# Two pairs of routed blocks at a time: one group of products a slot, and four blocks' weights in one tile

## The chip, the cores and the metric

One core of a Trainium2 chip runs the whole program. The metric is the device time of one execution in microseconds. Three runs of the kernel before took 1347.44, 1349.66 and 1351.03 us; the median, 1349.66 us, is the time to compare with. One further execution was profiled; every duration below is from it.

Engines are named as in the profile: PE is the matrix engine (PEld its weight loads), DVE the vector engine, ACT the scalar engine, POOL the general engine, SP the one that only issues transfers.

## What is computed

A transformer layer, once: attention between two layer norms, then a feed-forward layer with routed experts and a shared expert between two more. All of it is in float32.

```python
x = x + _layernorm(attn(_layernorm(x), wq, bq, wkv, bkv, wo))
x = x + _layernorm(ffn(_layernorm(x), gate_w, w_gate, w_up, w_down, sh_gate, sh_up, sh_down))
```

The input has 8 sequences of 512 rows of 256 values. Attention has 4 groups of 4 query heads of 128, with one key and one value head for each group, and a causal mask. The feed-forward layer is where the change lies:

```python
scores = softmax(x @ gate_w.T)                 # 64 experts
topk_w, topk_idx = top_k(scores, 6)
# expert e takes at most CAP = 64 of the rows that chose it, in order: buf[e] is 64 x 256
g = silu(einsum('ech,ehf->ecf', buf, w_gate))  # f = 176
u = einsum('ech,ehf->ecf', buf, w_up)
d = einsum('ecf,efh->ech', g * u, w_down)
y = (d of each row's six experts, weighed by topk_w, 0 for rows over CAP)
y = y + silu(x @ sh_gate.T) * (x @ sh_up.T) @ sh_down.T
```

Each expert's block is 64 rows, so two experts make a pair of 128 rows, and there are 32 pairs. Three weights of an expert (256 x 176, 256 x 176 and 176 x 256) are 176 KB each.

## The kernel before

**The loop.** Attention runs over 128 heads `k`: 16 a sequence, a "head" being four query heads' share of one tile of rows (line 1450). The order of all instructions on PE, DVE, ACT, POOL and SP is the program's own order: it is written out by hand (`manual_schedule`, line 176), and nothing is reordered. In each head the loop takes, in this order: the score products 3 and 2 (`scores`, L566, with a reduction on DVE, L570, and an exponential on ACT, L574), the exchange of the head before (`turned`, two transposes on DVE, L602, then four transfers to DRAM and one back into `et`), score products 1 and 0, the weighing on POOL (`weigh`, L584), query products (`queries`, L426), the products with the values for the head two before (`mix`, L639, evicted by ACT at L650), side work of the feed-forward layer, and keys or values of the next group (`group_step`: nothing, keys, values, values for heads 0, 1, 2, 3 mod 4).

**The routed experts between.** The experts' work is a generator, `experts` (L1056), and the loop takes a step of it (`next(routed)`) at up to four places of a head, called slots here:

- slot a, after `turned(k - 1)` and before score products 1 and 0 (L1467)
- slot b, after the weighing and before the queries (L1496)
- slot c, after `mix` (L1521)
- slot d, at the end of the head, after `group_step` (L1557)

Slots b and c are open from head 94, a and d from head 97's end. The first steps build the tables of rows (`tables`); then `experts` goes over pairs `m`, with two steps an iteration. The first step of iteration m holds `start_pair(m)`, `down(m - 5)`, `gate_up(m - 3)`, `turn_hidden(m - 4)`, `load_gate_up(m - 1)` and `load_down(m - 3)`; the second holds `gate_up_hidden(m - 3)`, `scatter(m - 5)`, `turn_rows(m - 2)` and a step of `free_slots`. What they do for one pair:

| step | lines | what it issues |
|---|---|---|
| `start_pair` | 948 | POOL: an indirect gather of the pair's 128 rows into `gx` |
| `load_gate_up`, `load_down` | 958, 965 | ACT queue: three transfers of 352 KB into `wgu` and `wd` |
| `turn_rows` | 973-977 | PE: two transposes (`ptx`); DVE: copies `gxt`, `gw` |
| `gate_up` | 984, 987 | PE: products of 64 columns for the two experts, side by side (`pgu`); ACT: tanh into `hid` |
| `gate_up_hidden` | 993, 994 | DVE: two operations on `hid` and `pgu` |
| `turn_hidden` | 1001, 1003 | PE: two transposes (`pth`); DVE: copy `ht` |
| `down` | 1010, 1018 | PE: products of 64 columns (`pd`); ACT: two scaled copies into `dd` |
| `scatter` | 1021 | POOL: an indirect transfer that adds `dd` to `y_d` |

**Buffers.** PSUM has three pools here: `ps_s` with three banks, shared by `psc`, `ptx`, `pth` and some of the shared expert's products; `ps_m` with three banks, shared by `pq`, `pav`, `pk`, `pv`, `pd`, `pgu` and others (`bank`, L74); `ps_o` for the output sums. In SBUF, pool `p3` has two buffers of each tag, so `wgu` and `wd` each hold two pairs, and `gxt` and `ht` two; `gx` and `dd` have three, `gw` four. Tags `wgu` and `wd` are also used by `join_heads` early in the program, and by `finish` after the routed work.

**After the routed work.** When `experts` sets `pairs["all"]`, the loop turns to `finish_early`, which adds up, normalises and stores the first five sequences.

Of the kernel before, what the change touches and what calls it, by code (L numbers as in the profile page):

```python
# [11 lines left out]
F32 = mybir.dt.float32  # L12
# [7 lines left out]
P = 128  # L20
B, T, E = 8, 512, 256
NT = B * T
NI = T // P
# [4 lines left out]
G, QPG, D = 4, 4, 128  # L28
NH = G * QPG
NX, F, TOPK, CAP = 64, 176, 6, 64  # L30
FC = F // 2
NM = NX // 2
# [7 lines left out]
EARLY = 5  # L40
# [7 lines left out]
def sandwich_kernel(ctx, tc, x, wq, bq_t, wkv, bk_t, bv, wo, gate_wt, w_gate, w_up, w_down,  # L48
                    sh_gate_t, sh_up_t, sh_down_t, pe_t, out):
    nc = tc.nc  # L50
# [23 lines left out]
    def bank(shape, name):  # L74
        return ps_m.tile(shape, F32, tag="m", name=name)
# [43 lines left out]
    def on_act(dst, src):  # L119
        nc.scalar.copy(dst, src)  # L120
# [35 lines left out]
    with ExitStack() as part:  # L156
# [785 lines left out]
        table, pairs = {}, {}  # L942

        def start_pair(m):

            l = pairs[m] = {"m": m}
            l["gx"] = p4[0].tile([P, ROW], F32, tag="gx", name=f"gx_{m}")
            nc.gpsimd.indirect_dma_start(
                out=l["gx"], out_offset=None, in_=xg_d[:, :],
                in_offset=bass.IndirectOffsetOnAxis(ap=table["idx"][:, m, 0:1], axis=0))  # L950

        def load_gate_up(key):
            l, queue = pairs[key], nc.sync if key == "late" else nc.scalar
            m = l["m"]

            l["wgu"] = p3.tile([P, 2, 2, 2, F], F32, name=f"wgu_{key}", **l.get("wgu_at", {"tag": "wgu"}))
            for k, w in enumerate((w_gate, w_up)):
                queue.dma_start(out=l["wgu"][:, :, k, :, :].rearrange("p e c f -> p e (c f)"),
                                in_=w[ds(m * 2, 2)].rearrange("e (p c) f -> p e (c f)", p=P))

        def load_down(key):
            l, queue = pairs[key], nc.sync if key == "late" else nc.scalar
            m = l["m"]
            l["wd"] = p3.tile([FC, 2, 2, E], F32, name=f"wd_{key}", **l.get("wd_at", {"tag": "wd"}))
            queue.dma_start(out=l["wd"].rearrange("p e c h -> p e (c h)"),
                            in_=w_down[ds(m * 2, 2)].rearrange("e (p c) h -> p e (c h)", p=FC))

        def turn_rows(key):
            l = pairs[key]
            pt = ps_s.tile([P, 2, P], F32, tag="s", name=f"ptx_{key}")  # L970
            rows = l["gx"][:, :E].rearrange("s (p c) -> s c p", c=2)
            for c in range(2):
                nc.tensor.transpose(pt[:, c, :], rows[:, c, :], ident)
# [16 lines left out]
        def gate_up_hidden(key):  # L990
            l = pairs[key]
            pgu = l.pop("pgu")
            nc.vector.scalar_tensor_tensor(l["hid"], l["hid"], 1.0, pgu[:, 0, :], ALU.add, ALU.mult)
            nc.vector.scalar_tensor_tensor(l["hid"], l["hid"], 0.5, pgu[:, 1, :], ALU.mult, ALU.mult)

        def turn_hidden(key):
# [5 lines left out]
            l["ht"] = p3.tile([FC, 2, P], F32, tag="ht", name=f"ht_{key}")  # L1002
            on_dve(l["ht"], pt[:FC])

        def down(key):
            l = pairs[key]
            pd = bank([P, E], f"pd_{key}")
            for c in range(2):
                for e in range(2):
                    nc.tensor.matmul(pd[ts(e, CAP), :], lhsT=l["ht"][:, c, ts(e, CAP)],  # L1010
                                     rhs=l["wd"][:, e, c, :], start=c == 0, stop=c == 1)
            dd = l["dd"] = p4[0].tile([P, E], F32, tag="dd", name=f"dd_{key}")
            if key == "late":
                on_act(dd, pd)
                return
            for e in range(2):
                rows = slice(e * CAP, (e + 1) * CAP)
                nc.scalar.mul(dd[rows, :], pd[rows, :], l["gw"][rows, e : e + 1])
# [37 lines left out]
        def experts():  # L1056


            yield from tables()
            yield  # L1060
            later = free_slots()
            for m in range(NM + 5):
                if m < NM:
                    start_pair(m)
                for behind_, step in ((5, down), (3, gate_up), (4, turn_hidden), (1, load_gate_up), (3, load_down)):
                    if 0 <= m - behind_ < NM:
                        step(m - behind_)
                yield
                if 0 <= m - 3 < NM:
                    gate_up_hidden(m - 3)  # L1070
                if 0 <= m - 5 < NM:
                    scatter(m - 5)
                if 0 <= m - 2 < NM:
                    turn_rows(m - 2)
                if m >= 2:
                    next(later, None)
                if m == NM + 4:
                    pairs["all"] = True
                yield

        def output(b, y, x1):
# [14 lines left out]
        def finish(b, tags):  # L1096

            ys = [q.tile([P, NI, E], F32, tag=tag, name=f"y{n}_{b}") for n, (q, tag) in enumerate(tags[:2])]
# [3 lines left out]
            x1 = residual(b, *tags[2])  # L1102
# [301 lines left out]
        EARLY_TAGS = [(p3, "wgu"), (p3, "wd")]  # L1404

        FINISHED_AT = (1, 2, 5, 6, 8)

        def finish_early():

            rows = [finish(b, EARLY_TAGS + [[(p1, "xn"), (p2, "xnt")][b % 2]]) for b in range(EARLY)]  # L1410

            def at(n, mixed):
                for b, first in reversed(list(enumerate(FINISHED_AT))):
                    if first <= n <= first + 3 if mixed else n in (first, first + 2):
                        next(rows[b])

            return at
# [32 lines left out]
        for k in range(NK):  # L1450
            b, s = divmod(k, NH)
# [76 lines left out]
            if k == FIRST_FREE:  # L1528

                work = table["work"]  # L1530
                table["rest"] = nc.values_load(work[0:1, 0:1], min_val=0, max_val=NM - 1)
                table["m"] = nc.values_load(work[0:1, 1:2], (ET.DVE, ET.SP), min_val=0, max_val=NM - 1)
                pairs["late"] = {"m": table["m"], "wgu_at": {"tag": "wgu_late", "bufs": 1},
                                 "wd_at": {"tag": "wd_late", "bufs": 1}}
                load_gate_up("late")
            if k == FIRST_FREE + 2:
                load_down("late")
# [36 lines left out]
        with tc.For_i(0, table["rest"], 1) as n:  # L1574
            m = nc.values_load(table["work"][0:1, ds(n + 2, 1)], (ET.DVE, ET.SP), min_val=0, max_val=NM - 1)
# [82 lines left out]
```

## Time and profile before

| what | us |
|---|---|
| median of three runs | 1349.66 |
| the profiled execution, its own time | 1346.28 |
| its span, first to last instruction | 1344.6 |
| first routed load issued / last `pd` product | 892.7 / 1167.0 |
| one `pd` product, one `pgu` product (mean length) | 0.38 / 0.46 |
| one `ht` copy, one `gxt` copy on DVE | 0.42 / 0.42 |
| one `tanh` on ACT, one scaled copy `dd` | 0.32 / 0.47 |

The granted clock of PE was 0.997 over the execution. A product's length runs from its start to its modelled end, and products overlap, so the time that one takes from the next is the distance between their starts: some 0.22 us for a 128x256 instruction of `pav` (0.38 us long), of which a float32 product has two. In the page's first part an engine's share is busy time over the span. In a timeline each line is a start, a length, the engine, the line of the kernel, the operation, what it writes and reads, its shape and how many were merged; in brackets stands idle time before it and what ended it.

### The profile page before, as it was taken

How to read it: one execution, taken by the hardware profiler on the slowest of the kernel's cores; microseconds unless marked ns; L12 is line 12 of the kernel's file. 1: busy time of each engine (PE TensorE's matmuls, PEld its weight loads, DVE VectorE, ACT ScalarE, POOL GpSimd, SP SyncE). 2: the span in 40 equal slices, each digit the busy share in tenths (PEclk: the TensorE clock that was granted, in tenths of full speed). 3: DMA queues.
4: the chain of work that ended last, by engine and by line, in shares of the span. 5: the costliest groups of instructions: out<-in, count | busy, mean ns of one | idle time of the engine just before them, and what ended most of it. 6: DMA issues, size and time to landing. Idle time of an engine off the chain costs nothing. (4 is left out here: it accounts for less than half of the span.)

```text
span 1344.6 us, 21778 instructions
## 1 busy us (share of the span) xinstructions
PE 1319.8 (98%) x6746; PEld 1018.7 (76%) x6746; DVE 911.5 (68%) x2931; ACT 546.8 (41%) x1665; POOL 660.3 (49%) x1080
## 2 busy tenths in 40 slices
PE   9999999999999999999999999999999999999997
PEld 7877887888778887788778877876667676767774
DVE  5575577777887678777886778666656444567645
ACT  3333354334443454344433443434343334444523
POOL 4556463436452563446434643355545444477711
PEclk9999999999999999999999999999999999999999
DMA  8676677756775676566765667579999889777712
GB/s 268 176 219 208 201 215 219 205 185 211 220 218 174 201 226 213 177 209 204 224 193 162 204 189 202 171 213 303 307 284 281 246 239 299 182 239 262 234 36 72
DMA packets 160435, 285.53 MB, mean 212 GB/s; under 512 B 17292, under 2 KB 123437, under 8 KB 160317
## 3 DMA queue, kind: packets, MB, share of 16 engines
q1 hardware_dynamic: 122893, 212.14, 52.6%
q0 software_dynamic: 13328, 36.05, 9.1%
q10 hardware_dynamic: 24096, 35.92, 8.5%
q8 instruction: 55, 0.90, 0.3%
q14 instruction: 63, 0.52, 0.1%
HBM read 168.44 MB, written 115.61 MB: 211 GB/s over the span
## 5 line engine op out<-in xcount | busy, mean ns | idle before, releaser
L584 POOL TENSOR_SCALAR e<-e,recip 128x512 f32<-128x512 f32 (+1 forms) x504 | 245.3, 525 | 424.1 <-DVE recip L580 367.7
L574 ACT ACTIVATE e<-e,least 128x32 f32<-128x32 f32 (+1 forms) x504 | 258.5, 514 | 260.4 <-DVE least L570 235.1
L639 PE MATMUL pav<-et,v 128*128 128x256 f32 x1280 | 300.4, 382 | 11.5 <-DMA et<-ex_d 8.9
L639 PEld LDWEIGHTS pav<-et,v 128*128 128x128 f32 x1280 | 241.5, 191 | 52.8 <-issue 7.1
L566 PE MATMUL psc<-kt,qt 128*128 128x32 f32 (+15 forms) x1024 | 274.9, 407 | 0.9 <-DVE qt L431 0.4
L570 DVE CUSTOM_DVE_ANT_0 e<-psc,mask 128x32 f32<-128x32 f32 (+1 forms) x504 | 204.2, 430 | 96.4 <-PE psc L566 93.8
L650 ACT ACTIVATE ao<-pav,bv_sb 128x256 f32<-128x256 f32 x255 | 107.1, 471 | 368.5 <-PE pav L639 344.7
L566 PEld LDWEIGHTS psc<-kt,qt 128*128 128x128 f32 x1024 | 161.5, 191 | 59.4 <-issue 25.9
L602 DVE STREAM_TRANSPOSE eb<-e 128x1024 f32<-128x1024 f32 (+1 forms) x252 | 197.5, 822 | 2.0 <-POOL e L584 1.5
L1021 POOL DMA_INDIRECT y_d<-dd,idx x32 | 51.1, 1597 | 93.2 <-ACT e L574 27.2
L574 ACT ACTIVATION_READ_ACCUMULATOR e<-e,least 128x1 f32 x504 | 94.6, 188 | 0.0
L716 PEld LDWEIGHTS pc<-set,crossed 128*128 128x128 f32 x640 | 77.0, 192 | 4.9 <-issue 1.7
L716 PE MATMUL pc<-set,crossed 128*128 128x128 f32 x640 | 78.8, 276 | 0.6 <-POOL crossed L710 0.6
L426 PE MATMUL pq<-xnt,wq_sb 128*128 128x256 f32 x320 | 75.5, 380 | 0.0
L716 PEld LDWEIGHTS ps<-set,ao 128*128 128x128 f32 x480 | 59.9, 192 | 15.3 <-issue 7.4
L470 PE MATMUL pq_back<-rows_joined,heads 128*128 128x256 f32 x264 | 71.3, 379 | 0.0
L388 PEld LDWEIGHTS pv<-wkv_sb,xnt 128*128 128x128 f32 x512 | 65.9, 192 | 4.5 <-issue 1.1
L388 PE MATMUL pv<-wkv_sb,xnt 128*128 128x128 f32 x512 | 67.5, 275 | 0.5 <-ACT ao L650 0.5
L426 PEld LDWEIGHTS pq<-xnt,wq_sb 128*128 128x128 f32 x320 | 59.2, 190 | 9.2 <-issue 0.7
L379 DVE SCALAR_TENSOR_TENSOR kt<-pk,bk_sb,pe_sb 128x512 f32<-128x512 f32 x32 | 24.0, 750 | 60.5 <-PE pk L377 58.5
L470 PEld LDWEIGHTS pq_back<-rows_joined,heads 128*128 128x128 f32 x264 | 50.2, 190 | 16.2 <-issue 8.2
L377 PE MATMUL pk<-xnt,wkv_sb 128*128 128x512 f32 x128 | 60.2, 593 | 0.3 <-ACT xnt L120 0.3
(281 smaller groups left out, 2017.6 us busy)
## 6 DMA issues: line engine op xcount, KB each, us to landing
ex_d<-eb SPq DMA_DIRECT2D x504, 160.0 KB
et<-ex_d SPq DMA_DIRECT2D x126, 640.0 KB
wgu<-in_w_gate ACTq DMA_DIRECT2D x32, 352.0 KB
wgu<-in_w_up ACTq DMA_DIRECT2D x32, 352.0 KB
wd<-in_w_down ACTq DMA_DIRECT2D x32, 352.0 KB
set<-wc_d SPq DMA_DIRECT2D x20, 512.0 KB
set<-ws_d SPq DMA_DIRECT2D x20, 384.0 KB
y<-y_d POOLq DMA_DIRECT2D x10, 512.0 KB, 6.8
```

Of the source, the lines that this page charges most:

```text
L377: nc.tensor.matmul(pk, lhsT=wkv_sb[:, c, g, 0, :], rhs=s["xnt"][:, c, :], start=c == 0, stop=c == NC - 1)
L388: nc.tensor.matmul(pv[:, i, :], lhsT=s["xnt"][:, c, ts(2 * n + i, P)], rhs=wkv_sb[:, c, g, 1, :], start=c == 0, stop=c == NC - 1, skip_gro ...
L426: nc.tensor.matmul(pq[:, n, :, :], lhsT=wq_sb[g][:, c, ts(2 * pair + n, D)], rhs=seqs[b]["xnt"][:, c, :].rearrange("p (u v) -> p u v", v=P ...
L470: nc.tensor.matmul(out, lhsT=factor[0], rhs=factor[1], start=first, stop=last, skip_group_check=True)
L566: nc.tensor.matmul(psc[:, :w], lhsT=halves[k // 2][:, at, :, :].rearrange("d h t -> d (h t)"), rhs=seqs[b]["kt"][g][:, :w], start=True, st ...
L570: nc.vector.tensor_tensor_reduce(out=e, in0=psc[:, :w].rearrange("p (c t) -> p c t", t=BS), in1=mask[:, T - w :].rearrange("p (c t) -> p c ...
L574: nc.scalar.activation(e, e, AF.Exp, bias=l["least"][:, q : q + 1], scale=-1.0, accum_out=l["total"][:, q : q + 1])
L584: engine.tensor_scalar(e, e, recip[:, q : q + 1], 1.0, ALU.mult, ALU.mult)
L602: nc.vector.transpose(eb[:, :, first : first + count, :, :].rearrange("p a j r t -> p j a r t"), weighed[k % 2][:, end - count : end, :, : ...
L639: nc.tensor.matmul(pav[n // NI][:, :, n % 2, :], lhsT=seqs[b]["v"][g][:, j, :], rhs=et[:, :, first + j, :], start=j == 0, stop=j == count ...
L650: nc.scalar.activation(ao, pav[n // NI][:, :, n % 2, :], AF.Identity, bias=bias)
L716: nc.tensor.matmul(bank_[:, n, :], lhsT=a, rhs=w, start=pair == 0 and n == 0, stop=pair == 1 and n == len(factors[0]) - 1, skip_group_chec ...
```

## The change

The 32 pairs become 16 twos of pairs.

- **Steps and slots.** `experts` now loops over n with four steps an iteration. Step one: `gate_up_hidden` for both pairs of n - 1, and one scatter of n - 2. Step two: `turn_hidden` for both pairs of n - 1. Step three: the other scatter, `turn_rows` for both pairs of n, `start_pair` for both of n + 1. Step four: the down products of n - 1, the gate and up products of both pairs of n, then the loads of gate and up for n + 1 and of down for n. Two steps stand ahead of the loop.
- **Down products** of two pairs write one bank `pd` of 128x2x256; four scaled copies follow.
- **Weights** of four blocks stand in one tile, with one buffer of each tag; gate, up and down each come in one transfer of 704 KB from ACT's queue. The late pairs keep their own loads.
- **`join_heads` and `finish`** use halves of one tile in place of two buffers of a tag.

```diff
@@ join_heads
-            t = p3.tile([P, 4, 2, D], F32, tag="wgu" if g >= 2 else "wd", name=f"heads_{g}")
+            tag = "wgu" if g >= 2 else "wd"
+            if tag not in joined:
+                joined[tag] = p3.tile([P, 2, 4, 2, D], F32, tag=tag, name=f"heads_{tag}", bufs=1)
+            t = joined[tag][:, g % 2]
...
+        def load_gate_up_of_two(n):
+            t = p3.tile([P, 4, 2, 2, F], F32, tag="wgu", name=f"wgu_{n}", bufs=1)
+            for k, w in enumerate((w_gate, w_up)):
+                nc.scalar.dma_start(out=t[:, :, k, :, :].rearrange("p e c f -> p e (c f)"),
+                                    in_=w[ds(n * 4, 4)].rearrange("e (p c) f -> p e (c f)", p=P))
+            for at in range(2):
+                pairs[2 * n + at]["wgu"] = t[:, 2 * at : 2 * at + 2]
+
+        def load_down_of_two(n):
+            t = p3.tile([FC, 4, 2, E], F32, tag="wd", name=f"wd_{n}", bufs=1)
+            nc.scalar.dma_start(out=t.rearrange("p e c h -> p e (c h)"),
+                                in_=w_down[ds(n * 4, 4)].rearrange("e (p c) h -> p e (c h)", p=FC))
...
+        def down_products(l, pd):
+            for c in range(2):
+                for e in range(2):
+                    nc.tensor.matmul(pd[ts(e, CAP)], lhsT=l["ht"][:, c, ts(e, CAP)], rhs=l["wd"][:, e, c, :],
+                                     start=c == 0, stop=c == 1, skip_group_check=True)
...
+        def down_two(n):
+            pd = bank([P, 2, E], f"pd_{n}")
+            for at in range(2):
+                down_products(pairs[2 * n + at], pd[:, at, :])
+            for at in range(2):
+                l = pairs[2 * n + at]
+                dd = l["dd"] = p4[0].tile([P, E], F32, tag="dd", name=f"dd_{2 * n + at}")
                 for e in range(2):
+                    rows = slice(e * CAP, (e + 1) * CAP)
+                    nc.scalar.mul(dd[rows, :], pd[rows, at, :], l["gw"][rows, e : e + 1])
...
@@ experts
-            for m in range(NM + 5):
-                if m < NM:
-                    start_pair(m)
-                for behind_, step in ((5, down), (3, gate_up), (4, turn_hidden), (1, load_gate_up), (3, load_down)):
-                    if 0 <= m - behind_ < NM:
-                        step(m - behind_)
...
+            two(0, start_pair)
+            yield
+            once(0, load_gate_up_of_two)
+            yield
+            for n in range(NM // 2 + 2):
+                two(n - 1, gate_up_hidden)
+                once(n - 2, lambda n: scatter(2 * n))
+                next(later, None)
                 yield
+                two(n - 1, turn_hidden)
+                yield
+                once(n - 2, lambda n: scatter(2 * n + 1))
+                two(n, turn_rows)
+                two(n + 1, start_pair)
+                next(later, None)
+                if n == NM // 2 + 1:
                     pairs["all"] = True
+                yield
+                once(n - 1, down_two)
+                two(n, gate_up)
+                once(n + 1, load_gate_up_of_two)
+                once(n, load_down_of_two)
                 yield
...
@@ finish_early
-            rows = [finish(b, EARLY_TAGS + [[(p1, "xn"), (p2, "xnt")][b % 2]]) for b in range(EARLY)]
+            both = [p3.tile([P, 2, NI, E], F32, tag=tag, name=f"early_{tag}", bufs=1) for tag in ("wgu", "wd")]
+            rows = [finish(b, [t[:, b % 2] for t in both], [(p1, "xn"), (p2, "xnt")][b % 2]) for b in range(EARLY)]
```

(`two(n, step)` takes a step for pairs 2n and 2n + 1, `once(n, step)` takes it for n; both do nothing outside the 16 twos.)

More of the change, by code (lines that the diff above doesn't have):

```diff
@@ L952, in load_gate_up @@
         def load_gate_up(key):
-            l, queue = pairs[key], nc.sync if key == "late" else nc.scalar
-            m = l["m"]
-            l["wgu"] = p3.tile([P, 2, 2, 2, F], F32, name=f"wgu_{key}", **l.get("wgu_at", {"tag": "wgu"}))
+            m = pairs[key]["m"]
+            t = pairs[key]["wgu"] = p3.tile([P, 2, 2, 2, F], F32, tag="wgu_late", name=f"wgu_{key}", bufs=1)
             for k, w in enumerate((w_gate, w_up)):
-                queue.dma_start(out=l["wgu"][:, :, k, :, :].rearrange("p e c f -> p e (c f)"),
-                                in_=w[ds(m * 2, 2)].rearrange("e (p c) f -> p e (c f)", p=P))
+                nc.sync.dma_start(out=t[:, :, k, :, :].rearrange("p e c f -> p e (c f)"),
+                                  in_=w[ds(m * 2, 2)].rearrange("e (p c) f -> p e (c f)", p=P))
@@ L961, in load_down @@
         def load_down(key):
[L962 to L966, printed above, removed]
+            m = pairs[key]["m"]
+            t = pairs[key]["wd"] = p3.tile([FC, 2, 2, E], F32, tag="wd_late", name=f"wd_{key}", bufs=1)
@@ new lines, in load_down @@
+            nc.sync.dma_start(out=t.rearrange("p e c h -> p e (c h)"),
+                              in_=w_down[ds(m * 2, 2)].rearrange("e (p c) h -> p e (c h)", p=FC))
+        def load_gate_up_of_two(n):
[5 more added lines that the diff above has]
+                pairs[2 * n + at]["wgu"] = t[:, 2 * at : 2 * at + 2]
@@ L968, in turn_rows @@
+        def load_down_of_two(n):
[3 more added lines that the diff above has]
+            for at in range(2):
+                pairs[2 * n + at]["wd"] = t[:, 2 * at : 2 * at + 2]
         def turn_rows(key):
@@ L1007, in down @@
             pd = bank([P, E], f"pd_{key}")
-            for c in range(2):
-                for e in range(2):
[L1010 to L1018, printed above, removed]
+            down_products(l, pd)
+            l["dd"] = p4[0].tile([P, E], F32, tag="dd", name=f"dd_{key}")
+            on_act(l["dd"], pd)
+        def down_two(n):
+            pd = bank([P, 2, E], f"pd_{n}")
+            for at in range(2):
+                down_products(pairs[2 * n + at], pd[:, at, :])
+            for at in range(2):
+                l = pairs[2 * n + at]
+                dd = l["dd"] = p4[0].tile([P, E], F32, tag="dd", name=f"dd_{2 * n + at}")
+                for e in range(2):
+                    rows = slice(e * CAP, (e + 1) * CAP)
+                    nc.scalar.mul(dd[rows, :], pd[rows, at, :], l["gw"][rows, e : e + 1])
         def scatter(m):
@@ L1061, in experts, with two, once @@
             later = free_slots()
-            for m in range(NM + 5):
-                if m < NM:
-                    start_pair(m)
-                for behind_, step in ((5, down), (3, gate_up), (4, turn_hidden), (1, load_gate_up), (3, load_down)):
-                    if 0 <= m - behind_ < NM:
-                        step(m - behind_)
-                yield
[L1069 to L1077, printed above, removed]
-                    pairs["all"] = True
+            def two(n, step):
+                if 0 <= n < NM // 2:
+                    for at in range(2):
+                        step(2 * n + at)
+            def once(n, step):
+                if 0 <= n < NM // 2:
+                    step(n)
+            two(0, start_pair)
[6 more added lines that the diff above has]
+                next(later, None)
+                yield
+                two(n - 1, turn_hidden)
[5 more added lines that the diff above has]
+                if n == NM // 2 + 1:
+                    pairs["all"] = True
+                yield
[3 more added lines that the diff above has]
+                once(n, load_down_of_two)
                 yield
@@ L1094, in output, with finish @@
             yield
-        def finish(b, tags):
-            ys = [q.tile([P, NI, E], F32, tag=tag, name=f"y{n}_{b}") for n, (q, tag) in enumerate(tags[:2])]
+        def finish(b, ys, room):
             for k in range(2):
@@ L1101, in finish @@
                 yield
-            x1 = residual(b, *tags[2])
+            x1 = residual(b, *room)
             for i in range(NI):
@@ L1401, in last_output @@
                     nc.sync.dma_start(out=rows_of(out, b * T)[:, i - 1 : i + 1, :], in_=x1[:, i - 1 : i + 1, :])
-        EARLY_TAGS = [(p3, "wgu"), (p3, "wd")]
         FINISHED_AT = (1, 2, 5, 6, 8)
         def finish_early():
-            rows = [finish(b, EARLY_TAGS + [[(p1, "xn"), (p2, "xnt")][b % 2]]) for b in range(EARLY)]
+            both = [p3.tile([P, 2, NI, E], F32, tag=tag, name=f"early_{tag}", bufs=1) for tag in ("wgu", "wd")]
+            rows = [finish(b, [t[:, b % 2] for t in both], [(p1, "xn"), (p2, "xnt")][b % 2]) for b in range(EARLY)]
             def at(n, mixed):
@@ L1532, in sandwich_kernel @@
                 table["m"] = nc.values_load(work[0:1, 1:2], (ET.DVE, ET.SP), min_val=0, max_val=NM - 1)
-                pairs["late"] = {"m": table["m"], "wgu_at": {"tag": "wgu_late", "bufs": 1},
-                                 "wd_at": {"tag": "wd_late", "bufs": 1}}
+                pairs["late"] = {"m": table["m"]}
                 load_gate_up("late")
```

## The prediction

> **What bounds the kernel now.** I read the page's busy shares first, then the routed stage in stretches of time (columns: stretch, length, busy time and instructions of PE, PEld, DVE, ACT, POOL, granted clock, DMA share, GB/s), then who waited for whom on PE, then the routed tiles, then one head's timeline.
>
> ```profile
> PE 1319.8 (98%) x6746; PEld 1018.7 (76%) x6746; DVE 911.5 (68%) x2931; ACT 546.8 (41%) x1665; POOL 660.3 (49%) x1080
> ...
> 880.00:1172.00 292.00, 287.86 (x1573) 200.46 (x1572) 163.14 (x555) 114.89 (x332) 143.52 (x177) 1.00 0.89 263
> ...
> 940.00:980.00 40.00, 39.00 (x205) 26.30 (x202) 22.33 (x69) 14.93 (x40) 19.83 (x24) 1.00 0.99 305
> ...
> PE pav L639 <- DMA et<-ex_d: 2.8, 2, 1.8
> ```
>
> TensorE sets the end: 98% over all, 287.9 of 292 us in the routed stage, where its only named waits above 1 us are two for `et` (2.8 us together). The DMA engines come second, full from 940 to 980. VectorE is at 56%, but its order is written by hand, so its place in a chain can matter although its share doesn't. So a term counts if it changes PE's own time or makes PE wait.
>
> PE and then DVE around one step between two heads (start, duration, what, count):
>
> ```profile
> 1015.00 1.08 PE L1010 MATMUL pd<-wd,ht 88*64 88x256 f32 x8
> 1015.92 1.35 PE L984 MATMUL pgu<-wgu,gxt 128*64 128x352 f32 x8
> 1017.20 0.46 PE L1001 MATMUL pth<-ident,hid 128*88 128x128 f32 x2
> 1017.50 0.76 PE L566 MATMUL psc<-kt,qt 128*128 128x160 f32 x4
> 1018.18 0.51 PE L973 MATMUL ptx<-ident,gx 128*128 128x128 f32 x2
> 1018.52 1.40 PE L566 MATMUL psc<-kt,qt 128*128 128x352 f32 x4
> ...
> 1018.04 0.31 DVE L570 CUSTOM_DVE_ANT_0 e<-psc,mask 128x160 f32<-128x160 f32 x1
> ...
> 1018.30 0.36 DVE L570 CUSTOM_DVE_ANT_0 e<-psc,mask 128x192 f32<-128x192 f32 x1
> ...
> 1018.58 1.57 DVE L602 STREAM_TRANSPOSE eb<-e 128x1024 f32<-128x1024 f32 x2
> 1020.07 0.30 DVE L993 SCALAR_TENSOR_TENSOR hid<-hid,pgu 128x176 f32<-128x176 f32 x1
> 1020.40 0.34 DVE L994 SCALAR_TENSOR_TENSOR hid<-hid,pgu 128x176 f32<-128x176 f32 x1
> 1020.66 0.42 DVE L123 COPY gxt<-ptx 128x256 f32<-128x256 f32 x1
> ...
> 1021.06 0.52 DVE L570 CUSTOM_DVE_ANT_0 e<-psc,mask 128x352 f32<-128x352 f32 x1
> ```
>
> Two things are to be seen. The score and transpose outputs share three PSUM banks in turn (pool `ps_s`), so each needs the bank of the one three places earlier: `ptx` at 1018.18 needs that of `pth`, and starts just after `ht` was copied out. And DVE puts the 1.57 us transpose L602 between the second and third score reduction. Today the last two score products don't mind: their banks are those of the first two, reduced before L602. They run underneath it.
>
> **Slots.** The steps are taken four at a time in a head k: a (between scores 2 and 1), b (before the queries), c (after `mix`), d (end). Counting yields, old and new both begin after six table slots and end in head 115. Before, down and gate/up products of one pair stand in b and d of each head; afterwards those of two pairs stand in c alone, `gate_up_hidden` in d, `turn_hidden` in a, `turn_rows` in b.
>
> **1. Fewer groups of half-width products.** From the starts of consecutive PE instructions in the trace: the full-width instruction before `pd` lasts 94 ns longer to the next start than its like (523 for 429 ns), the first `pd` pair 51 longer, the last `pgu` 101 longer (389 for 288), the first `pth` 78 longer (187 for 109; `pth_late`, which follows no such group, has none). 0.324 us a group. There are 34 groups (30 joint, 2 of gate/up alone, 2 of down alone), then 17: 17 x 0.324 = **-5.5 us**. The products themselves stay: 0.21 us per `pd` pair of instructions, 0.29 per `pgu` pair.
>
> **2. Slot a: the wait that takes their place.** PE's order becomes psc3, psc2, pth, pth, psc1, psc0 on three banks. psc0 needs the bank of the first `pth`, hence its copy `ht`, and DVE's order is reduce 3, reduce 2, L602, `ht`, `ht`. From the start R of reduce 3, psc0 can start at R + (reductions 0.26 to 0.76 by width) + 1.49 + 0.42 + 0.05. PE has only psc1 (0.5 to 0.8 us) and the transposes (0.11 each) to do meanwhile. Any of the three banks is released only behind L602, so another rotation would not help.
>
> R is late too. Let T be the end of the last `pgu`. ACT first copies four `dd` (0.95 a pair, from 0.25 after `pd`, thus until T-0.2), then two `tanh`; the second can't start before T+0.18. DVE's two `hid` pairs (0.65 each) then end at T+1.5; where the key product stands between (heads 2 mod 4) its `kt` (0.75, ready at T+1.9) comes first and they end at T+3.9. DVE reduces only after that. Ends of psc0, less PE's pure work, less what the old slot a lost anyway (elapsed time between psc3's start and psc0's end, against its products):
>
> - heads 1 mod 4 (no keys or values between): 4.58 - 2.33 - 0.37 = 1.9
> - 2 mod 4 (keys): 7.04 - 4.00 - 0.20 = 2.8
> - 3 mod 4 (values 0.87): 4.75 - 3.12 - 0.13 = 1.5
> - 0 mod 4 (values): 4.56 - 3.13 - 0.64 = 0.8
>
> 7.0 for four heads, and slot a carries `turn_hidden` in the 16 heads 99 to 114: **+28 us**. If `hid` is never late, R follows psc3 alone: 0.75 + 1.1 + 1.4 + 0.4 = 3.65 for four, +14.6: the lower bound. Above, 32 (side steps' DVE work ahead of `hid`). Behind psc0 on PE stands all of the head, so nothing gives it back but the 2.8 us of waits for `et`.
>
> Here a rule speaks against the change: the Trainium skill (Perfetto Trace Analysis, Optimization Strategy) reads a gap that repeats on the saturated engine as too little PSUM or SBUF for the next tile. By the row, the three `ps_s` banks cost 2.9 us in 12 of today's `ptx`; by the rule, two more transposes between scores on the same three should make it a regular bubble, of a size it doesn't tell.
>
> **3. Banks of the other pool.** Slot c takes all three `ps_m` banks: `pd`, `pgu`, `pgu`. The second `pgu` needs that of `pav`: two ACT evictions, 0.84 us together, against 2.9 us of products before it. Keys or values need that of `pd`: four `dd` end 2.2 us after it, PE comes at 2.4. Taken at **0**; covered by 2.1 and 0.2 us, and 0.2 x 16 = 3 us if the last slips.
>
> **4. Weights.** Transfers from ACT go from 96 to 48 of twice the size, bytes and run lengths alike. ACT's issue takes 374 to 482 ns each, at times up to 1704; ACT is 39% busy, and PE's next need of it is half a head away: 0. But one buffer for four blocks means that the loads start only after the last `pgu` of the slot, and `wd`, last in its queue, is wanted first. Counting the queue's bytes in the trace, now gate and up land 3.1 to 7.8 us after the first issue, the second 1.1 us behind the first, and `wd` 2.1 to 5 behind that; all are there 1.9 to 13 us ahead of use. Doubled: up + 2 x 1.1 + 2 x (wd - up) = 9.6 to 16.8, mean 12.3 (an estimate). They are wanted at interval - 4.3 (the products of slot c) + the stalls of 2. Intervals between ends of `mix` are 13.5 to 21.8, first 11.1: wanted after 10.5 to 20. A wait of some 3 us at the first load, 1 us in six or seven short heads. Bounds 0 and 15; I take **+5**, the lower half, as DMA gains from every pause of PE.
>
> The Trainium skill (DMA: Bandwidth & Descriptors, Anatomy of one DMA; Rules for kernel authors) gives a software-issued transfer a fixed 2 us and asks for 1 MiB or more in one. By that, 48 transfers fewer would save 96 us of transfer time; by this trace no product waits for a weight, and the saving is nothing.
>
> **5. The rest at nothing.** 32 gathers and 32 scatters stay; POOL issues two gathers in a row in b, about 1.0 us each, with half of POOL's time free. `join_heads` and the early `finish` write the same bytes into parts of one tile instead of two; their readers and the order are the same. No PE wait stands there to be had, so no gain either.
>
> **Sum.** -5.5 + 28 + 0 + 5 = +27.5. On the profiled execution's 1346.28 (span 1344.6 and 1.7 around it) 1373.8; that execution lies 3.4 below the median of the runs, so on 1349.66: **1377 us**, slower by 2%.
>
> **Rivals.**
> - *Faster*: the wait in slot a doesn't arise and only the 5.5 us remain, 1344. For: DVE is 56% busy, and every step is still there one slot ahead of its user. Against: it needs L602 and `ht` within psc1's time, 1.95 us in at most 0.8. It decides below that point. 9%, with a tenth of no change beside it (4%).
> - *`hid` is in time* (other PE work in d hides it): -5.5 + 14.6 = +9, 1359. Against: heads 1 mod 4 have nothing between. 18%.
> - *Weights bind*: the 2.1 MB burst lands at 12.3 to 16.8 after T in most heads, each waits 1 to 2 us more than taken, +43 with the other terms, 1393. For: DMA at 0.99 from 940 to 980. Against: PE's new pauses lengthen the head. 12%.
> - *The group isn't one group*: the second `pgu` waits for `pav`'s eviction, the saving is gone, +33, 1383. Against: 2.1 us of cover. 5%.
> - *Forecast*: 52%; its own range runs from +14.6 - 5.5 - 2.8 = +6 to 32 - 5.5 + 15 = +42.
>
> Three runs spread over 0.27%, so 0.3% is what this kernel's measurement tells from no change. Faster 9%, same 4%, slower 87%. The range of 8 in 10 leaves out the fast case and the top of the weights': 1357 to 1393.
>
> **What would show it.** Step 1: 17 starts of `pgu` groups with 16 products each, each preceded by `pd`. Step 2: psc0 starting within 0.1 us of the end of the first `ht` copy in every head 99 to 114, and idle PE of 1 to 3 us there; psc0 right behind psc1 would refute it. `hid` ending before `psc3` would point to the second rival. Step 4: PE idle before `pd` ended by a DMA. A PE busy share in the stage no lower than now would make the prediction wrong.

## The result and the profile after

The changed kernel takes **1395.1 us** in the median of 6 runs (1389.95 to 1407.97), beside 1348.55 for the kernel before on the same chip: a ratio of **1.0357 [1.0302, 1.0412]**, slower, and 2 us above the top of the predicted range. The profiled execution took 1389.95 us with a span of 1387.9, 43.3 more than before's. It was the fastest of the six, at a granted clock of 0.992; the two slowest took 1403.55 and 1407.97 us at 0.983 and 0.984, so the waits below are those of an execution 5 us under the median.

From the page, the busy shares and the group of the score products (count, then busy time and mean ns of one, then idle time before them and what ended most of it); lines below the change have moved, L566 is now L569, L570 is L573, L602 is L605, L1010 is L1023, L984 is L999, L639 is L642, L973 is L988, L1001 is L1016:

```profile
PE 1329.1 (96%) x6746; PEld 1025.5 (74%) x6746; DVE 914.9 (66%) x2931; ACT 549.0 (40%) x1665; POOL 659.8 (48%) x1080
...
L569 PE MATMUL psc<-kt,qt 128*128 128x32 f32 (+15 forms) x1024 | 282.7, 412 | 17.6 <-DVE ht L123 15.0
```

The view of stretches over the routed stage (stretch, length, busy time and instructions of PE, PEld, DVE, ACT, POOL, granted clock, DMA share, GB/s):

```profile
880.00:1215.00 335.00, 297.99 (x1583) 208.75 (x1582) 166.99 (x559) 117.54 (x334) 145.45 (x180) 0.98 0.79 231
940.00:980.00 40.00, 35.47 (x192) 23.37 (x187) 18.88 (x61) 14.16 (x38) 19.67 (x22) 0.96 0.87 254
```

And who waited for whom on PE in it (total, times, longest):

```profile
PE psc L569 <- DVE ht L123: 15.0, 16, 1.3
PE pd L1023 <- DMA wd<-in_w_down: 9.8, 7, 2.0
PE pth L1016 <- DVE least L573: 5.7, 9, 1.7
PE pth L1016 <- DVE hid L1009: 3.4, 4, 0.9
```

The instructions on PE are as many as before, and PE went from 287.9 of 292 us to 298.0 of 335. Where DMA stood at 0.99 between 940 and 980, it stands at 0.87. Two waits are new and large: scores behind `ht` 16 times, once in each head that carries `turn_hidden`, and down products behind `wd` in seven. The waits for `et` of before are gone. One head on PE and then on DVE shows the first, slot a:

```profile
1081.58 0.56 PE L569 MATMUL psc<-kt,qt 128*128 128x32 f32 x4
1081.97 0.67 PE L1016 MATMUL pth<-ident,hid 128*88 128x128 f32 x4
1082.47 1.06 PE L569 MATMUL psc<-kt,qt 128*128 128x480 f32 x2
1084.31 1.12 PE L569 MATMUL psc<-kt,qt 128*128 128x512 f32 x2 [0.78 <-DVE ht L123]
```

```profile
1082.17 0.22 DVE L573 CUSTOM_DVE_ANT_0 e<-psc,mask 128x64 f32<-128x64 f32 x1
...
1082.38 1.57 DVE L605 STREAM_TRANSPOSE eb<-e 128x768 f32<-128x768 f32 x2
1083.87 0.71 DVE L123 COPY ht<-pth 88x256 f32<-88x256 f32 x2
```

`ht` stands behind the transpose L605 on DVE; its first copy, half of the pair of 0.71 us, ends near 1084.3, and there psc0 starts.

**Where the 43.3 us are.** I took the start-to-start distances of consecutive PE instructions from the end of `mix` in head 95 to its end in head 114, and subtracted what each takes when nothing holds it (261.8 us in both kernels). The stretch grew from 285.7 to 326.8 us, by 41.1; the part ahead of it grew by 2.1, and the part behind it by 0.1.

| lost time on PE, us | before | after | difference |
|---|---|---|---|
| slot a: around `psc`, `pth`, `ptx` | 5.9 | 37.8 | +31.9 |
| `pd` behind `wd` | 0 | 10.3 | +10.3 |
| granted clock at half | 0 | 6.1 | +6.1 |
| second `pgu` behind `dd` | 0.2 | 1.2 | +1.0 |
| switches of groups of half-width products | 10.3 | 5.2 | -5.1 |
| waits for `et` and the table products | 3.9 | 0 | -3.9 |
| the rest | 3.6 | 4.4 | +0.8 |

This says where PE stood, not what it would gain if one row went. The experiments ask that.

### The profile page after: what moved, and what is told of

It is laid out like the page before. It is cut to its first block, busy times and chain, and to the rows that moved or that the text cites. A ratio compares the mean times of both kernels' runs of the same rounds, so it can differ in the third digit from the quotient of the medians.

```text
span 1387.9 us, 21650 instructions
## 1 busy us (share of the span) xinstructions
PE 1329.1 (96%) x6746; PEld 1025.5 (74%) x6746; DVE 914.9 (66%) x2931; ACT 549.0 (40%) x1665; POOL 659.8 (48%) x1080
## 5 line engine op out<-in xcount | busy, mean ns | idle before, releaser
L587 POOL TENSOR_SCALAR e<-e,recip 128x512 f32<-128x512 f32 (+1 forms) x504 | 241.4, 495 | 512.9 <-DVE recip L583 450.9
L642 PE MATMUL pav<-et,v 128*128 128x256 f32 x1280 | 300.2, 382 | 8.5 <-DMA et<-ex_d 6.3
L569 PE MATMUL psc<-kt,qt 128*128 128x32 f32 (+15 forms) x1024 | 282.7, 412 | 17.6 <-DVE ht L123 15.0
L642 PEld LDWEIGHTS pav<-et,v 128*128 128x128 f32 x1280 | 241.5, 191 | 49.1 <-issue 4.9
L573 DVE CUSTOM_DVE_ANT_0 e<-psc,mask 128x32 f32<-128x32 f32 (+1 forms) x504 | 205.3, 430 | 109.6 <-PE psc L569 106.7
L569 PEld LDWEIGHTS psc<-kt,qt 128*128 128x128 f32 x1024 | 161.4, 191 | 86.0 <-issue 26.2
L605 DVE STREAM_TRANSPOSE eb<-e 128x1024 f32<-128x1024 f32 (+1 forms) x252 | 197.5, 822 | 2.1 <-POOL e L587 1.5
L719 PE MATMUL ps<-set,ao 128*128 128x128 f32 x480 | 60.0, 275 | 0.0
L667 PE MATMUL po<-wo,ao 128*128 128x256 f32 x240 | 59.4, 387 | 0.0
```

Of the source, the lines that this page charges most:

```text
L569: nc.tensor.matmul(psc[:, :w], lhsT=halves[k // 2][:, at, :, :].rearrange("d h t -> d (h t)"), rhs=seqs[b]["kt"][g][:, :w], start=True, st ...
L573: nc.vector.tensor_tensor_reduce(out=e, in0=psc[:, :w].rearrange("p (c t) -> p c t", t=BS), in1=mask[:, T - w :].rearrange("p (c t) -> p c ...
L587: engine.tensor_scalar(e, e, recip[:, q : q + 1], 1.0, ALU.mult, ALU.mult)
L605: nc.vector.transpose(eb[:, :, first : first + count, :, :].rearrange("p a j r t -> p j a r t"), weighed[k % 2][:, end - count : end, :, : ...
L642: nc.tensor.matmul(pav[n // NI][:, :, n % 2, :], lhsT=seqs[b]["v"][g][:, j, :], rhs=et[:, :, first + j, :], start=j == 0, stop=j == count ...
L667: nc.tensor.matmul(po[b][i // 2][:, i % 2, :], lhsT=ao[:, h, :], rhs=whole[j // 2][h], start=n == 0 and h == 0, stop=n // 2 == G - 1 and h ...
```

## The experiments

Ratios are against the kernel before on the same chip.

### One part of the change at a time

**Slot a, two ways.** The first puts the slot ahead of L605 in DVE's order, so `ht` no longer stands behind the transposes; the second gives `pth` a bank of the other pool.

```diff
+            if twice and not finishing:
+                next(routed, None)
             if 0 <= k - 1 < NK - 2:
                 turned(k - 1)
-            if twice and not finishing:
-                next(routed, None)
```

> The changed kernel with slot a taken before turned(k - 1): the two copies ht come ahead of the transposes L602 on DVE, all else as in the change. Order theory (psc0 waits for ht, which stands behind L602): the 16 waits of psc for ht (15.0 us in the trace after) fall below 3 us, the waits of pth for hid and for the reductions stay (some 9 us); time 1395 - 15 = 1380, or some 5 less if the clock's half windows go too. Weights theory (single buffer of weights is the main cost): within 3 us of 1395. Clock theory (the half clock is the main cost, whatever makes PE pause): 1395 less at most the 6 us of the half windows.

```diff
-            pt = ps_s.tile([P, 2, P], F32, tag="s", name=f"pth_{key}")
+            pt = bank([P, 2, P], f"pth_{key}") if key != "late" else ps_s.tile(
...
```

> The changed kernel with the pth of the routed pairs in pool ps_m instead of ps_s; no instruction moves. Bank theory: psc0 then needs the bank of psc3, so the waits of psc for ht (15.0 us) and of pth for the reductions (5.7 us) go, the waits of pth for hid (3.4 us) stay or grow to 5; time 1395 - 18 = 1377, some 5 less if the half windows of the clock go with them. If it is DVE's order alone and not the bank, or the weights: within 4 us of 1395. If ps_m is too short of banks now, pq or pav wait in place of psc and the time stays.

Measured: 1394.47 us, 1.0348 [1.0307, 1.0389], and 1394.75 us, 1.0328 [1.0297, 1.0359]. Both edits did to the wait what they were to do, and neither moved the time; that is what both expectations named for the case that the weights bind. The waits on PE in the stage, first with the slot ahead of the transposes:

```profile
PE pd L1023 <- DMA wd<-in_w_down: 23.7, 9, 4.2
...
PE psc L569 <- DVE ht L123: 0.2, 1, 0.2
```

then with the other bank:

```profile
PE pd L1023 <- DMA wd<-in_w_down: 20.1, 9, 3.3
PE pth L1016 <- DVE hid L1009: 6.5, 13, 0.9
```

With the slot moved, 15.0 us of `ht` became 0.2, and 9.8 us of `wd` became 23.7; with the other bank `ht` is gone from this list for `psc`, and `wd` stands at 20.1. So about as much time is lost later in the head, at the weights, as was gained in slot a. The Trainium skill (Perfetto Trace Analysis, Optimization Strategy) says that a gap repeating on the engine that should be saturated can mean too little SBUF or PSUM for the next tile. That fits this wait, as the other bank ends it (and so does the other order on DVE), but says nothing of what the bank brings: here nothing at first, for the reason that the runs without loads show below.

**`hid` first, and `wd` first.** The first lets `gate_up_hidden` go ahead of the keys in slot d. The second issues `wd`'s load right behind the down products, ahead of the gate and up products and their loads.

```diff
+            twice = active and k > EARLY * NH + NH
+            if twice and not finishing:
+                next(routed, None)
             if k not in (2, 3):
                 group_step(k)
...
```

> The changed kernel with slot d taken before group_step, so that the two hid pairs stand ahead of kt on DVE; PE's order is the same. My step 2 put 2.4 us of the lateness in each of the four heads 2 mod 4 on kt: if so, those four heads lose 2 us less each, time 1395 - 8 = 1387, and the waits of pth for hid (3.4 us, 4 times) go. If hid is late because of the four dd copies and two tanh on ACT ahead of it, the time stays within 3 us of 1395.

```diff
                 once(n - 1, down_two)
+                once(n, load_down_of_two)
                 two(n, gate_up)
                 once(n + 1, load_gate_up_of_two)
-                once(n, load_down_of_two)
```

> The changed kernel with the load of wd issued right after the down products, ahead of the gate and up products and their loads, so that it is first in its queue and not last. Weights theory: pd's waits for wd (9.8 us, 7 times) go below 1 us; gate and up land later by 3 to 6 us and are wanted 1.8 us later, so up to 4 us of new waits before pgu; time 1395 - 8 = 1387. If the DMA engines are simply full in that stretch, the waits move from pd to pgu and the time stays within 3 us of 1395.

Measured: 1390.87 us, 1.0303 [1.027, 1.0335], where `pth` behind `hid` went from 3.4 to 0.8 us and `pd` behind `wd` from 9.8 to 12.9; and **1383.1** us, 1.0242 [1.0211, 1.0273], where no product waits for `wd` any more:

```profile
PE psc L569 <- DVE ht L123: 15.0, 16, 1.3
...
PE pgu L999 <- DMA wgu<-in_w_up: 3.8, 4, 1.3
```

So the order of the three loads is worth some 12 us, more than the 8 that I expected, and `hid` 4 at most; slot a's 15 us stand as they were.

### Slot a and the weights together

If the two are parallel, only both at once should bring much. Four kernels: other bank and `wd` first; these and `hid` first; one more empty slot ahead of the loop, so that all steps stand a quarter of a head later (products in d, `hid` in a, `turn_hidden` in b); and this with `wd` first.

> Both edits together: pth of the routed pairs in ps_m, and wd loaded right after the down products. Each alone moved the time by 0 and -12 us, and with the first alone pd's waits for wd grew from 9.8 to 20.1 us. Two floors in parallel (the order of slot a, and the chain gate/up products, load, land, down products of the next head): only together do they come down; the waits of psc for ht and of pd for wd both stay below 2 us, some 4 to 8 us of waits for hid, dd and wgu remain; time 1395 - 15 - 10 - 5 (clock) = 1365. If a third thing (the DMA engines being full) is the floor: not below 1380.

> As pool_wd, and slot d ahead of group_step, so that hid doesn't stand behind kt. Two-floors theory: the waits of pth for hid (6.5 us, 13 times with the other pool) shrink to about 3, time some 3 us below pool_wd. If hid is late by ACT's order (four dd, two tanh), no change against pool_wd.

```diff
             once(0, load_gate_up_of_two)
             yield
+            yield
             for n in range(NM // 2 + 2):
```

> The changed kernel with one more yield ahead of the loop: every step one slot later (products in d, hid in a behind L602, pth in b, ptx in c). Slot theory: nothing that psc needs stands behind L602 now, so the waits of psc for ht and of pth for hid go; the weights' chain is untouched, so pd's waits for wd grow to 20 us or more as in the two runs that took slot a's waits away; time 1385 to 1395. If the weights don't bind by themselves: 1365 or less.

> One slot later, and wd loaded right after the down products. Two-floors theory: both floors down, waits of a few us for wgu and banks, the 5.3 us of fewer switches stay saved: 1350 to 1358. If the waits only move on (wgu in place of wd, the banks of ps_m held from d to a in place of those of ps_s): 1375 or more.

Measured: bank and `wd` 1378.29, 1.0223 [1.0185, 1.0261]; all three 1376.3, 1.0207 [1.016, 1.0253]; shifted 1395.32, 1.0358 [1.0318, 1.0399]; shifted and `wd` first **1371.46**, 1.0189 [1.0144, 1.0233]. The shifted kernel again has no wait for `ht` in slot a and again the same time, with 27.5 us behind `wd` (10 times) and 13.0 at half clock. Together the two bring 17 to 24 us, not the 30 to 45 that I expected. With bank and `wd` these are the largest waits left:

```profile
PE ptx L988 <- DMA gx<-xg_d,idx: 7.8, 6, 2.3
PE pgu L999 <- DMA wgu<-in_w_up: 6.4, 4, 2.3
PE pth L1016 <- DVE hid L1009: 6.1, 12, 0.9
PE pav L642 <- DMA et<-ex_d: 2.9, 1, 2.9
```

Three of the four are for transfers: gathers (`gx`), gate and up weights, and `et`. So PE still waits for transfers, but no longer for one load alone.

### Without the loads

Each of these leaves out all loads of routed weights but the first and computes every group with those, so its output isn't the layer's; only its time is of use. They are the kernel before, the kernel after, and after with the other bank for `pth`.

```diff
-            t = p3.tile([P, 4, 2, 2, F], F32, tag="wgu", name=f"wgu_{n}", bufs=1)
-            for k, w in enumerate((w_gate, w_up)):
+            t = kept["wgu"] = kept.get("wgu") or p3.tile([P, 4, 2, 2, F], F32, tag="wgu", name=f"wgu_{n}", bufs=1)
+            for k, w in () if n else enumerate((w_gate, w_up)):
...
```

> The kernel before, but from the third pair on no routed weights are loaded: every pair uses the weights of one of the first two. It is the base for the two runs beside it. No product waits for a weight in the kernel before, so only the DMA time that is freed can show: the two waits for et (2.8 us) go, time 1349 - 3 = 1346, by either theory.

> The changed kernel without its weight loads after the first four blocks (all later products use these). Two-floors theory: what is left is slot a's floor alone, its waits (some 32 us over the kernel before), less 5.3 us of switches, plus 0 to 5 us of half clock: 1346 + 27 to 32 = 1373 to 1378. If the weights are the only floor and slot a's waits are hidden behind them: 1350 or less.

> The changed kernel without weight loads and with pth of the routed pairs in ps_m. Two-floors theory: both floors gone, the 5.3 us of fewer switches left against some 8 us of waits for hid and dd: 1345 to 1352. If slot c is a floor by something else than weights and banks (ACT's four dd, the gathers): 1360 or more.

Measured: 1345.48, 0.9973 [0.9959, 0.9987]; 1376.87, 1.0194 [1.0153, 1.0235]; 1353.81, 1.0039 [1.002, 1.0058]. In a table, us:

| | with all loads | first loads only |
|---|---|---|
| before | 1349.2 | 1345.5 |
| after | 1395.1 | 1376.9 |
| after, other bank for `pth` | 1394.8 | 1353.8 |

The medians of the kernel before lay between 1348.5 and 1350.4 us on all the chips used, so the table's times can be compared. Read by rows, the loads cost 4 us before, 18 after, and **41** once slot a doesn't wait. Read by columns, slot a costs 0 with the loads and **23** without. That is the picture of two chains side by side: either alone keeps the time up, and only both gone bring it down. The two runs of the kernel after came out as the two-floors theory expected (1373 to 1378) and 2 us above it (1345 to 1352). The waits of PE without loads, in the kernel after, and then with the other bank (lines behind the loads stand one further down here):

```profile
PE psc L569 <- DVE ht L123: 14.3, 16, 1.0
PE pth L1017 <- DVE hid L1010: 4.6, 7, 1.0
```

```profile
PE pth L1017 <- DVE hid L1010: 6.6, 16, 0.9
PE pav L642 <- DMA et<-ex_d: 2.4, 1, 2.4
```

The weights' chain in the kernel after: `pgu` ends, three loads of 704 KB go, the last packet of `wd` lands 11.7 us after the first issue (mean, 10.5 to 12.9) and its signal comes at 12.1 (11.3 to 13.6), and the down, gate and up products of the next head take 4.3 us before the buffers are free again. With 0.1 us at each end that is some 16.5 us from the last `pgu` of one head to that of the next. Of 15 turns, the seven whose `pd` waited for `wd` took 15.8 to 17.2 us, but for one of 18.9 with half clock in it.

A mean hides what this does. Without loads and with the other bank the 15 turns take 13.3 to 22.6 us, 16.1 in the mean, so the chain looks harmless. But the same seven lie between 13.3 and 14.5: at 16.5 each they would be 19 us longer in all (an estimate), and `pd` waits 20.1 us for `wd` with that bank. The other eight have 16.0 us or more of their own. Split in this way, in us:

| turns from last `pgu` to last `pgu` | seven short | eight long |
|---|---|---|
| first loads only, other bank | 96.7 | 144.7 |
| first loads only | 106.2 | 158.9 |
| all loads | 117.8 | 160.4 |
| all loads, other bank | 129.9 | 152.3 |

With all loads, the other bank does gain 8 us, in the long turns, where the weights are early. It loses 12 in the short ones: there the half clock stood for 20.5 us in place of 3.4, which is up to 8.5 of the 12 (half of the difference, an estimate). So the unchanged time is a gain and a loss that happen to cancel; why the short turns lost the other 3 to 4 us isn't taken apart.

Even with neither, the new steps cost 1353.8 - 1345.5 = 8.3 us more than the old: 6.6 us behind `hid` in 16 heads and some 4 in smaller waits, against some 5 saved at the switches. The 2.4 us behind `et` aren't part of it, as the kernel before has 2.7 without its loads; the rest, 2 to 3 us, has no row.

### The one tile, or the moment of the loads?

The steps of the change with the loads of before: a tile and two buffers for each pair, each load issued behind its own pair's products. Alone, with the other bank, with `hid` first besides, and shifted by a slot.

```diff
+                once(n - 1, down_two)
+                two(n, load_down)
+                for at in range(2):
+                    if n < NM // 2:
+                        gate_up(2 * n + at)
+                    if n + 1 < NM // 2:
+                        load_gate_up(2 * n + 2 + at)
```

> The change's steps and slots, but the weights as in the kernel before: a tile a pair, two buffers, three transfers of 352 KB a pair, each pair's loads issued as soon as that pair's products are through, wd right after the down products. Slot a stays as in the change. If the one tile with three transfers is what makes the weights late, their waits go as in the kernel before: time as without loads, 1373 to 1380. If it is that the products of two pairs stand in one slot (so that all loads start at its end, in whatever tiles), the time is that of the changed kernel with wd first, 1380 to 1386, with waits for wgu of 2 to 4 us.

> The change's steps and slots with a tile of weights a pair, each pair's loads behind its own products, and pth in ps_m: both floors relieved without touching the DMA total. If the weights' floor is the one tile and its place in the queue: some 5 us over the run without loads and with the same bank, 1355 to 1362. If it is that all loads of a head start within one slot (the DMA engines idle for a part of each head and full in another): as pool_wd or little below, 1368 to 1378, with waits for gx, et or wgu of 10 us or more.

> As pair_loads_pool, with slot d ahead of group_step. By the difference of all3 and pool_wd (2 us) some 2 to 4 us less than pair_loads_pool by either theory; the waits of pth for hid go below 3 us.

> The change's steps one slot later, a tile of weights a pair. Against shift1_wd (1371, with 10.7 us of waits for wgu): one-tile theory: these waits go, 1358 to 1362; bunched-loads theory: 1366 to 1371.

Measured: 1380.66, 1.0224 [1.019, 1.0259]; 1376.28, 1.0187 [1.0164, 1.021]; 1372.79, 1.0176 [1.014, 1.0213]; 1371.77, 1.0151 [1.0129, 1.0173]. Alone, own tiles end the waits for `wd` and leave 0.6 us for `wgu`, and the time is within 4 us of the run without loads (1376.9): there slot a is the longer chain, and the time lies at the border of the two theories' ranges. With the other bank the time is within 2 us of the same kernel with the one tile and `wd` first (1378.29), and 22 over the run without loads (1353.8), in the range expected for bunched loads. The waits on PE with own tiles and the other bank, and then ACT's lines of one head (these kernels are edits of the kernel before, so their lines up to 1018 are numbered as there):

```profile
PE ptx L973 <- DMA gx<-xg_d,idx: 8.0, 7, 1.7
PE pth L1001 <- DVE hid L994: 6.5, 15, 0.9
PE psg L1176 <- ACT v L120: 4.4, 2, 2.5
```

```profile
1044.68 0.45 ACTq L958 DMA_DIRECT2D wgu<-in_w_gate  x1
1051.25 0.38 ACTq L958 DMA_DIRECT2D wgu<-in_w_up  x1
1051.67 0.59 ACT L120 COPY gt<-pgt 128x512 f32<-128x512 f32 x1 [6.75 <-DMA wd<-in_w_down]
1052.15 0.38 ACT L120 COPY v<-pv 128x256 f32<-128x256 f32 x1
```

ACT was idle for 6.75 us, 6.1 of them between the issue of gate and that of up, and went on when a `wd` had landed. The packed trace tells why. The transfers of ACT and SP count on eight semaphores (100 to 107) in turn, and an issue waits until the semaphore that it takes is free. The one that up takes at 1051.25 belonged to the transfer of `wd` issued at 1042.38, and its last step stands at 1051.23. Behind the issue stood the copies of `gt` and of `v`, and PE waited 2.5 us for `v`.

Such stands between two issues come only with own tiles, which issue six loads in one slot; the kernels with one tile issue three, and the kernel before three in each of two slots. They are 5.2 us in two stands alone, 10.7 in three with the other bank, 7.3 in two with `hid` first, and 23.6 in six with the steps shifted. In the stage of the kernel before, and of those with one tile, there is none over 0.4 us. In the shifted one the two largest waits of PE, 5.8 and 4.6 us, follow them. The first, from ACT's issues over DVE to PE:

```profile
975.56 0.37 ACTq L958 DMA_DIRECT2D wgu<-in_w_gate  x1
982.93 0.37 ACTq L958 DMA_DIRECT2D wgu<-in_w_up  x1
985.56 0.18 DVE L580 RECIPROCAL recip<-total 128x4 f32<-128x4 f32 x1 [9.73 <-ACT e L574]
988.16 1.12 PE L973 MATMUL ptx<-ident,gx 128*128 128x128 f32 x4 [5.78 <-DVE hid L1193]
```

The issue at 982.93 stood 7.0 us for a transfer that it had nothing to do with: `x<-in_x`, issued by SP at 970.32, whose semaphore counted its last step at 982.91.

So equal times with one tile and with own tiles don't clear the one tile: own tiles bring a cost of their own, on ACT. Own tiles without these stands were not run.

What the loads are late for differs by kernel: `wd`, then gate and up, then gathers and `et`, and ACT itself. In bins of one microsecond between heads 97 and 112, counted from the packets, the DMA engines were below half busy in some 12 of 245 us before, 45 of 281 after, 37 of 273 with bank and `wd` first, and 33 of 266 with own tiles and bank (a few more or less by where the bins begin). Their mean share over the same stretches was 0.93, 0.81, 0.87 and 0.87. The kernel before left them 7% idle, so a part of a head in which they idle is hard to make up. I call this bunching of the loads into one slot a likely cause of the 22 to 25 us that the loads still cost with the other bank, with ACT's stands a part of it where the tiles are own. Neither is shown: no run spread the loads over the head under the new steps, and a second buffer for four blocks wasn't tried. No version with all its loads beat the kernel before; the best took 1371.5 and 1371.8 us.

## The prediction, step by step

- **Step 1 (-5.5)** holds: 5.1 us were saved at the switches, in 17 groups. **Step 3 (0)** came to 1.0 us, within its bound of 3: one `pgu` was late behind `dd` (0.9 us), not the keys or values that the step named.
- **Step 2 (+28)** holds as to place and, nearly, size: 31.9. All 16 heads show psc0 within 0.1 us of the end of the first `ht` copy. `hid` ended at T + 1.1 to 1.4 in ten heads (1.5 predicted), at T + 3.9 in three of the four with keys (3.9 predicted), and at T + 4.8 in the fourth; that one and two heads with side work (T + 2.1 and 3.8) are the excess. The 2.8 us for `et` came back as foreseen.
- **Step 4 (+5) failed**, at "the lower half, as DMA gains from every pause of PE". Its landing was right, 11.7 us for 12.3, and its own list, 3 us at the first load and 1 us in six or seven heads, gave 9 to 10; 10.3 was measured, with 0.7 us at the first load and 1.1 to 2.0 in six heads. Halving it had no row behind it: landings stayed at 10.5 to 12.9 us though PE paused in every head, and the loads start only when the products that read the buffer are done. The 96 us of transfer time that the step quotes weren't there to save either: the figure is for software-issued transfers, and the profile lists these loads' queue as hardware_dynamic (q10, 34.61 MB in the stage before, the bytes of the 96 loads).
- **The half clock (+6.1)** stood in no term. It came with the pauses.
- **The sum** nearly closes as an account of where PE stood: 27.5, and 3.9 for slot a, 5.3 for the weights, 6.1 for the clock, 2.1 ahead of the stage, 1.0 for `dd`, 0.8 for the rest, 0.4 for the switches, less 3.9 for `et` and the table products, give 43.2 of the 43.3. As a reason it was incomplete, because it set slot a and the weights beside each other as if each could be taken away. Slot a's cost is real, 23 us without the loads, but with them the time without slot a's wait is the same, 1394.8; the loads cost 18 us beside slot a and 41 without it.
- **The third rival** (weights bind, 1393) names the other chain, but its price, 2 us from the result, is luck. It wanted some 20 us at the weights, from loads that land at 12.3 to 16.8 us in most heads; they landed at 10.5 to 12.9, and 10.3 us were lost there.
- **The second rival** (`hid` in time, 1359) is refuted twice: `hid` was late as computed, and with `hid` first the time was 1390.9. The fast rival is refuted by the 15.0 us of `ht`.

## What to carry to other kernels

When a change takes away the room in which loads ran ahead, work out that loop by itself, from the last reader over the landing to the next last reader, and compare it with each turn, not with the mean: here some 16.5 us against a mean of 16.1 looks harmless, and yet seven turns of 13.3 to 14.5 us had to stretch. Two new waits on one engine are not a sum until you know that they don't share the same slack; the trial that shows it takes away each alone and both together. A wait that goes from 15.0 to 0.2 us at an unchanged time says that another floor is near. And when two versions take the same time, look whether they wait for the same thing before you call the difference between them harmless.

## What the runs showed of the hardware

**Half clock after short pauses.** Four times in the stage the granted clock fell to 0.50 for 3.41 us; in the stage of the kernel before it never did. One of them, on PE (a pause for `wd`, then products at half speed) and as stretches around it:

```profile
1167.18 3.24 PE L1023 MATMUL pd<-wd,ht 88*64 88x256 f32 x16 [2.04 <-DMA wd<-in_w_down]
```

```profile
1164.00:1167.70 3.70, 1.66 (x12) 1.12 (x12) 0.00 (x0) 0.84 (x2) 2.99 (x3) 1.00 0.78 204
1167.70:1171.10 3.40, 3.40 (x18) 2.26 (x16) 0.00 (x0) 0.58 (x2) 0.00 (x0) 0.50 0.74 242
```

The sixteen `pd` products took 3.24 us here and 1.95 in the head around 1074. The half clock begins behind a stretch of 3.7 us in which PE was idle for 2.04; before another (at 1041.4) two pauses stood, of 1.73 and 1.33 us. The four falls lie on one grid of 3.41 us, 22, 6 and 31 steps apart, and a grid step with 1.4 to 2.4 us of idle PE preceded each. Idle time in the step isn't all that decides: one with 1.75 us (ending at 1150.6) had no fall behind it. The Trainium skill (TensorE: Matmul & The Clock Gate, Why this matters for your kernels) warns of gaps above some 3 us, one idle window; here falls came behind pauses of 2.04 us and less. It cost 6.1 us in the changed kernel and 12.9 with the other bank for `pth`, where the waits for `wd` are longer: a part of what made that edit worth nothing.

**An engine behind its own issue.** The prediction priced the issues on ACT by their own 374 to 482 ns and so at nothing. That held with three loads in a slot. With six, an issue at times stood until an earlier transfer, even one of SP's, had landed and freed its semaphore: up to 7.0 us in one stand, with all of ACT's work behind it late. The 13 such issues started 0.02 to 0.03 us behind that semaphore's last step. Not every row that names a transfer is such a stand. In the trace of before, three rows put 11.8 us of ACT's idle time down to loads of weights; but there the issues had gone out over 3 us earlier, and each `ao` started 0.04 us behind the end of the `pav` products that it reads. Other heads have the same idle time of 3.95 us with `pav` named.
